# The two additions that complete the scores, as TensorE products into the bank of the transposed scores

## The chip, the cores and the metric

The kernel runs on one core of a Trainium2 chip. The metric is the time of one execution on the device, in microseconds, and the figure that counts is the median of several executions. In the profile, PE is TensorE (PEld its loading of the stationary operand), DVE is VectorE, ACT is ScalarE, POOL is GpSimd, and SP is the queue that issues most plain DMAs.

## The reference

Two graph layers over 3327 nodes with 128 features. The adjacency matrix is a mask times random weights, about 64 entries in a row, symmetric in its pattern. Layer 0 is a graph attention with four heads, and nearly all the time goes into it:

```python
def _gatv2_head(x, A_shape, w1, w2, a, Wlin):
    x1 = x @ w1
    x2 = x @ w2
    E = leaky_relu(x1[:, None, :] + x2[None, :, :], negative_slope=0.01)
    s = E @ a
    s = tanh(s / 8.0) * 8.0
    s = exp(s) * A_shape
    s = s / sum(s, axis=-1)
    out = s @ x @ Wlin.T
    return leaky_relu(out, negative_slope=0.01)

h = maximum(layernorm(x), 0);  x = x + concat(heads(h), axis=-1) @ w      # layer 0
h = maximum(layernorm(x), 0);  x = x + relu(A_norm @ (h @ W.T + b))        # layer 1
```

The score of a pair of nodes (i, j) in a head splits into a part with a relu and two plain terms: `leaky_relu(u) = 0.01 u + 0.99 relu(u)` with `u = x1[i] + x2[j]`, so `s = 0.99 a.relu(u) + 0.01 a.x1[i] + 0.01 a.x2[j]`. The last two are one number for each (j, head) and one for each (i, head). The change is about how these two numbers are added before the tanh.

## The kernel before, in words

**Tiling.** Rows are padded to 3328 and taken in 26 blocks of 128. A block is done in two halves (`hb`) of 64 rows. For each row the positions of its neighbours are found first, by `prep(b, k)`, and the neighbours' rows of a table in DRAM are then gathered. A half has four *words* `w` of eight tiles (`WT = 8`; a tile `g[:, t]` has 128 partitions, one pair (i, j) in each, with the features of j, the four plain terms of j at column `f0 + D`, and `x2[j]` for the four heads), and one *overflow word* (`w == NW`, three tiles, `ge`) for rows with more neighbours. That makes 26 x 2 x 5 = 260 words, 208 full ones and 52 overflow ones.

**Stages of a word.** `stage_z` works in groups `m` of four tiles, two groups to a full word: TensorE transposes the gathered `x2[j]` into PSUM (L622, 16 transposes for a group, in two halves `hp` of two heads), and VectorE takes the maximum with `-x1[i]` (L638, tile `r`). `stage_r` multiplies `r` with the attention vector on TensorE (L657): the relu parts of the scores stand in PSUM with pairs along the free axis. `finish` then turns scores into weights. It is a generator that does a piece of work, yields, and goes on at the next slot:

1. L666 ACT copies the scores to SBUF (`ssb`); L670 DVE makes `wq`.
2. Two slots later, L675: TensorE transposes `ssb` (four transposes of 128x128, three in an overflow word) into one bank `tr`, of which there are two for all users (`ps_tr`, `bufs=2`).
3. One slot later, L678: DVE adds to the transposed scores the plain term of j, which lies in `g`, into `sc` in SBUF; L681: DVE adds the term of i, which is `k.pex` in a full word and a part of `k.ex` in an overflow word.
4. Two slots later, L686 and L688: ACT takes tanh and exp of `sc`.
5. Two slots later, L697 (L715 in an overflow word): DVE multiplies by the adjacency weights into `wt`.
6. Five slots later, L706 (L724): TensorE accumulates `wt.T @ g` into `ag`, and `allow("g")` gives the gather buffer back to POOL's queue (L595).

`k.pex` is made once for a block at the end of `prep`: L561 DVE spreads the terms of i into `pmx` (each row's term under a mask), L566 TensorE multiplies with `modsel`, a 0/1 matrix that brings each row's term to the partitions of its pairs, and L568 ACT copies the product to SBUF.

**Order.** The instruction streams are written out in the order in which the Python code calls them (`manual_schedule`), and each engine runs its own stream in order. `slot()` is called six times for each group: before the group, after each half of the transposes of each `hp`, and after `stage_r`. Each call steps every open `finish` and `close` by one yield, steps `prep` of the next block at a fixed pace (72 steps in a block's 108 slots), and lets POOL issue gathers. So the DVE stream holds, between two of the L638 operations, whatever the slots between them put there. A PE instruction that waits holds up all PE instructions behind it, and the same goes for the other engines.

**L622 and its banks.** `z` has two buffers of two banks each, one for either `hp`. The transposes of one `hp` may start when L638 of the same `hp` one group earlier has read its bank.

The parts that the change touches: `prep` from L560 to L570, `finish` from L672 to L688.

Of the kernel before, what the change touches and what calls it, by code (L numbers as in the profile page):

```python
# [9 lines left out]
F32 = mybir.dt.float32  # L10
AF = mybir.ActivationFunctionType
OP = mybir.AluOpType
# [3 lines left out]
P = 128  # L16
SLOPE = 0.01
CAP = 8.0
# [44 lines left out]
OVT = 3  # L63
# [168 lines left out]
def _sparse_layers(tc, nc, x, adj, w1, w2, a, wlin, w, gw, gb, gb_sb, gwT, x_sb, dinv, flag, ident, out):  # L232
# [13 lines left out]
    NP, D = x.shape  # L246
    H = w1.shape[0]
# [5 lines left out]
    WT = 8  # L253
    NW = NT // WT
    LATE = 1

    with ExitStack() as l0:
# [19 lines left out]
        modsel = res.tile([P, P], F32, name="modsel")  # L277
# [8 lines left out]
        pb = l0.enter_context(tc.tile_pool(name="pb", bufs=2))  # L286
# [41 lines left out]
        def bank():  # L328
            return ps_tr.tile([P, 4, P], F32, name="tr").rearrange("p a b -> p (a b)")
# [23 lines left out]
        def prep(b, k):  # L353
# [114 lines left out]
            pm = bank()  # L468
# [27 lines left out]
            pm = bank()  # L496
# [22 lines left out]
            pm = bank()  # L519
            ex_ps = pm[:, :2 * OVT * 46].rearrange("p (t c) -> p t c", c=46)  # L520
            for c in range(2):
                for t in range(FOUND):
                    nc.tensor.matmul(ex_ps[:, OVT * c + t, :], oi[:, (FOUND * c + t) * P:(FOUND * c + t + 1) * P], ext[:, :46],
                                     start=True, stop=True)
# [25 lines left out]
            pm = bank()  # L550
            nc.tensor.matmul(pm, hTb, w1_sb.rearrange("p h d -> p (h d)"), start=True, stop=True)
            x1b = pb.tile([P, H * D], F32, name="x1b")
            nc.scalar.copy(x1b, pm)
            yield
            pm = bank()
            for h in range(H):
                nc.tensor.matmul(pm[:, h * P:(h + 1) * P], w1_sb[:, h, :], hTb, start=True, stop=True)
            x1n = pb.tile([P, H, P], F32, name="x1n")
            nc.scalar.activation(x1n, pm[:, :H * P].rearrange("p (h i) -> p h i", h=H), AF.Copy, scale=-1.0)
            pmx = pb.tile([P, 16, H], F32, name="pmx", bufs=1)  # L560
            nc.vector.tensor_tensor(pmx, tmask[:, :, None].to_broadcast([P, 16, H]),  # L561
                                    p_all[:, b, None, :H].to_broadcast([P, 16, H]), OP.mult)
            yield
            yield
            pm = bank()
            nc.tensor.matmul(pm[:, :16 * H], modsel, pmx.rearrange("p t h -> p (t h)"), start=True, stop=True)  # L566
            pex = pb.tile([P, 16, H], F32, name="pex")
            nc.scalar.copy(pex, pm[:, :16 * H].rearrange("p (t h) -> p t h", h=H))  # L568
            k.x1b, k.x1n, k.pex = x1b, x1n, pex
            yield  # L570

        def rows_in():
# [88 lines left out]
        def finish(k, hb, w):  # L661
            g, s = k.g.pop((hb, w)), k.s
            f0 = k.f0[hb]
            nt, nk, nm = (WT, 4, 2) if w < NW else (OVT, OVT, 1)
            ssb = ph.tile([P, BANK], F32, name="ssb", bufs=1)
            nc.scalar.copy(ssb[:, :nk * P], s[:, :nk * P])  # L666
            if w < NW:
                wq = pb.tile([P, WT, 8], F32, name="wq")
                diag = bass.AP(g.tensor, g.offset + BODY * hb, [list(g.ap[0]), [WIDE + 8, 8], [1, 8]])
                nc.vector.tensor_tensor(wq, diag, qmask[:, None, :].to_broadcast([P, WT, 8]), OP.mult)  # L670
            yield
            yield  # L672
            pt = ps_tr.tile([P, 4, P], F32, name="tr")
            for q in range(nk):
                nc.tensor.transpose(pt[:, q, :], ssb[:, q * P:(q + 1) * P], ident)  # L675
            yield
            sc = pb.tile([P, WT, H], F32, name="sc")
            nc.vector.tensor_tensor(sc[:, :nt].rearrange("p (m k) h -> p m k h", m=nm),  # L678
                                    pt.rearrange("p k (h m) -> p m k h", m=32)[:, :nm, :nk],
                                    g[:, :, f0 + D:f0 + D + H].rearrange("p (m k) h -> p m k h", m=nm), OP.add)  # L680
            nc.vector.tensor_add(sc[:, :nt], sc[:, :nt], k.pex[:, 8 * hb:8 * hb + 8] if w < NW else  # L681
                                 k.ex[:, OVT * hb:OVT * hb + OVT, 42:42 + H])
            yield
            yield
            th = pb.tile([P, WT, H], F32, name="th")
            nc.scalar.activation(th[:, :nt], sc[:, :nt], AF.Tanh, scale=1.0 / CAP)  # L686
            pe = pb.tile([P, WT, H], F32, name="pe")
            nc.scalar.activation(pe[:, :nt], th[:, :nt], AF.Exp, scale=CAP)  # L688
            yield
            yield  # L690

            if w == 0:
                k.ag = ps_a.tile([P, 2, 256], F32, name="ag")
            ag = k.ag
            if w < NW:
                wt = pv.tile([P, WT, H, 8], F32, name="wt", bufs=2)
                nc.vector.tensor_tensor(wt, pe[:, :, :, None].to_broadcast([P, WT, H, 8]),  # L697
                                        wq[:, :, None, :].to_broadcast([P, WT, H, 8]), OP.mult)
                yield
                yield  # L700
                yield
                yield
                yield
                for t in range(WT):
                    u, cg = t // 4, t % 4
                    nc.tensor.matmul(ag[32 * cg:32 * cg + 32, u, :WORK], wt[:, t].rearrange("p h q -> p (h q)"),  # L706
                                     g[:, t, f0:f0 + WORK], start=(w == 0 and t < 4), stop=False, skip_group_check=True)
                allow("g")
                return
            am = pb.tile([P, OVT, HALF], F32, name="am", bufs=1)  # L710
            wo = pv.tile([P, OVT, 8, H, 8], F32, name="wo")
            for t in range(OVT):
                nc.vector.scalar_tensor_tensor(am[:, t, :], code[:, :HALF], k.ex[:, OVT * hb + t, 41:42], g[:, t, BODY * hb:BODY * hb + HALF],
                                               op0=OP.is_equal, op1=OP.mult)
                nc.vector.tensor_tensor(wo[:, t], pe[:, t, None, :, None].to_broadcast([P, 8, H, 8]),  # L715
                                        am[:, t].rearrange("p (g q) -> p g q", q=8)[:, :, None, :].to_broadcast([P, 8, H, 8]), OP.mult)
                yield
            yield
            yield
            yield  # L720
            yield
            for t in range(OVT):
                for u in range(2):
                    nc.tensor.matmul(ag[:, u, :WORK], wo[:, t, 4 * u:4 * u + 4].rearrange("p g h q -> p (g h q)"),  # L724
                                     g[:, t, f0:f0 + WORK], start=False, stop=(t == OVT - 1), skip_group_check=True)
            allow("ge")
            tails.append(close(k, hb))
# [75 lines left out]
        for b in range(NB):  # L803
            k = Blk()
# [6 lines left out]
        SLOTP = 6 * 2 * NG  # L811
        AHEAD = 0.5
        preps = [prep(b, blks[b]) for b in range(NB)]
        queue = deque()
        done = [0] * NB
# [29 lines left out]
        def allow(kind):  # L845
            state[kind] += 1
# [345 lines left out]
        with tc.manual_schedule():  # L1192
# [5 lines left out]
            def scores(i):  # L1198
                if 0 <= i < n:
                    b, hb, m = groups[i]  # L1200
                    stage_r(blks[b], hb, m, rs.pop(i))
                    if m % 2 or m == NG - 1:
                        ends.append(finish(blks[b], hb, m // 2))
                    slot()

            for i in range(-1, n + 1):
                if i + 1 < n:
                    slot()
                if 0 <= i < n:
                    b, hb, m = groups[i]  # L1210
# [153 lines left out]
```

## Time and profile before

| | us |
|---|---|
| median of 9 runs | 3395.31 |
| lowest and highest of the 9 | 3378.94, 3409.59 |
| the profiled execution, its time | 3405.43 |
| its span, from the first to the last instruction | 3403.7 |
| PE matmul, busy | 2621.2 (77%) |
| DVE, busy | 2101.5 (62%) |
| ACT, busy | 682.7 (20%) |
| POOL, busy | 1714.7 (50%) |
| granted TensorE clock, mean | 0.887 |

How to read it: the profile has each instruction's start and duration by engine, source line and tile. A busy PE is the union of the matmuls' times, and a matmul's end is modelled, so of a run of matmuls the distance between starts tells what one takes in the stream, and the time of one (some 270 ns at full clock) is the way through the array. An fp32 matmul that isn't a transpose is two passes, each with its own load of the stationary operand, and is counted as two. The granted clock is either full or half over stretches of 3.4 us and more; the 0.887 is their mean. The chain is followed back from the last instruction to whatever released each, so its shares say which work the end waited for.

Over most of the span the picture is even: in 300 us stretches from 400 to 3100 us, PE is busy for 228 to 236 us, DVE for 184 to 196 us and ACT for 57 to 66 us.

### The profile page before, as it was taken

What the parts mean: (1) busy time and instruction counts of PE and PEld (TensorE: products, weight loads), DVE (VectorE), ACT (ScalarE), POOL (GpSimd) and SP (SyncE); (2) the same over time, 40 slices, a digit from 0 to 9 for tenths busy, and PEclk for the clock granted to TensorE, in tenths of its full rate; (3) what the DMA queues carried; (4) which work ended last, traced back from release to release, by engine and by line L of the source; (5) the groups of instructions that cost most, each with busy time, mean ns of one, the idle gap of its engine ahead of it and who ended that gap; (6) DMA issues with size and microseconds to landing.
All of it is one profiled execution on the core that took longest, in us unless ns stands there. A gap on an engine that the chain in (4) does not pass through costs nothing.

```text
span 3403.7 us, 52385 instructions
## 1 busy us (share of the span) xinstructions
PE 2621.2 (77%) x19410; PEld 1829.9 (54%) x19410; DVE 2101.5 (62%) x6426; ACT 682.7 (20%) x1703; POOL 1714.7 (50%) x1822
## 2 busy tenths in 40 slices
PE   6587777777887877777777777677777777787887
PEld 4355545555554555555555555555555555555543
DVE  6576666666666666666666665665665665665442
ACT  3122122112211212211221121221221121121110
POOL 3555555555455555545545545545555455445530
PEclk8798888888888989988888988988898888888999
DMA  9977677678677777877767867767777776777886
GB/s 324 320 252 259 207 259 255 217 243 281 211 240 260 239 234 257 262 215 247 257 196 251 269 202 246 258 205 242 249 229 230 240 227 219 247 219 228 257 281 186
DMA packets 417844, 826.94 MB, mean 243 GB/s; under 512 B 38435, under 2 KB 288815, under 8 KB 414255
## 3 DMA queue, kind: packets, MB, share of 16 engines
q0 software_dynamic: 141440, 619.41, 55.7%
q1 hardware_dynamic: 165343, 147.87, 14.0%
q10 hardware_dynamic: 110800, 56.25, 5.6%
q8 instruction: 156, 2.56, 0.3%
q14 instruction: 105, 0.86, 0.1%
HBM read 754.47 MB, written 113.22 MB: 255 GB/s over the span
## 4 chain that ended last, share of the span: by engine, by line
PE 50%; DVE 18%; issue 11%; another core or an unknown queue 11%; DMA 5%; POOL 4%; ACT 1%; SPq 0%; ACTq 0%; DVEq 0%; POOLq 0%
PE z L622 18%; PE s L657 10%; DVE r L638 9%; PE ag L706 4%; POOL g L595 4%; PE z L627 3%; PE tr L675 2%; DMA g<-table,idx 2%; DVE cand L422 2%; PE ag L724 2%; PE tr L379 2%; DVE codes L410 1%; PE z L988 1%; PE tr L757 1%
## 5 line engine op out<-in xcount | busy, mean ns | idle before, releaser
L595 POOL DMA_INDIRECT g<-table,idx x1664 | 1590.0, 956 | 1371.9 <-PE ag L706 802.2
L638 DVE TENSOR_TENSOR r<-z,x1n 128x1024 f32<-128x1024 f32 x832 | 1013.1, 1218 | 854.0 <-remote 341.7
L622 PE MATMUL z<-ident,g 128*128 128x128 f32 x6656 | 1044.6, 301 | 184.6 <-issue 117.3
L622 PEld LDWEIGHTS z<-ident,g 128*128 128x128 f32 x6656 | 850.8, 156 | 366.2 <-issue 236.0
L657 PE MATMUL s<-r,sel 128*2 128x512 f32 (+1 forms) x3744 | 552.7, 608 | 135.5 <-DVE r L638 91.6
L666 ACT COPY ssb<-s 128x512 f32<-128x512 f32 x260 | 146.9, 565 | 842.1 <-PE s L657 305.1
L706 PE MATMUL ag<-g,wt 128*32 128x133 f32 x3328 | 233.6, 307 | 95.2 <-issue 94.4
L657 PEld LDWEIGHTS s<-r,sel 128*2 128x2 f32 x3744 | 82.8, 84 | 411.2 <-issue 272.7
L706 PEld LDWEIGHTS ag<-g,wt 128*32 128x32 f32 x3328 | 134.1, 118 | 213.8 <-issue 204.4
L675 PE MATMUL tr<-ident,ssb 128*128 128x128 f32 x988 | 169.1, 296 | 92.5 <-issue 72.7
L422 DVE MAX8 cand<-codes 128x8 f32<-128x52 uint16 x1664 | 217.3, 204 | 0.0
L675 PEld LDWEIGHTS tr<-ident,ssb 128*128 128x128 f32 x988 | 127.2, 153 | 117.9 <-issue 93.3
L595 POOL DMA_INDIRECT ge<-table,idxo x104 | 101.1, 972 | 170.4 <-PE ag L724 81.3
L379 PE MATMUL tr<-at,x_sb 128*128 128x128 f32 x488 | 97.9, 357 | 113.9 <-ACT at L367 103.5
L367 ACT COPY at<-tr 128x512 f32<-128x512 f32 (+1 forms) x175 | 97.3, 556 | 409.4 <-remote 208.0
L686 ACT ACTIVATE th<-sc 128x32 f32<-128x32 f32 x260 | 58.4, 225 | 516.6 <-DVE sc L681 259.4
L379 PEld LDWEIGHTS tr<-at,x_sb 128*128 128x128 f32 x488 | 82.2, 252 | 141.6 <-ACT at L367 122.9
L633 DVE TENSOR_TENSOR r<-z,x1n 128x128 f32<-128x128 f32 x104 | 30.2, 290 | 192.3 <-PE z L627 140.7
L365 PE MATMUL tr<-ident,adjb 128*128 128x128 f32 x676 | 123.8, 311 | 27.7 <-DMA adjb<-in_adj_dram 16.3
L627 PE MATMUL z<-oi,x1b 128*128 128x256 f32 x416 | 133.2, 404 | 4.6 <-issue 4.6
L453 DVE MAX8 lists<-cand 128x8 f32<-128x272 f32 (+1 forms) x338 | 133.2, 394 | 2.2
L622 PE MATMUL z<-ident,ge 128*128 128x128 f32 x416 | 87.7, 286 | 43.0 <-issue 32.7
(199 smaller groups left out, 2611.1 us busy)
## 6 DMA issues: line engine op xcount, KB each, us to landing
adjb<-in_adj_dram SPq DMA_DIRECT2D x26, 1664.0 KB
table<-AT_d SPq DMA_DIRECT2D x26, 1664.0 KB
AT_d<-at ACTq DMA_DIRECT2D x150, 256.0 KB
g<-table,idx POOLq DMA_INDIRECT x1664
table<-img SPq DMA_DIRECT2D x12, 1296.0 KB
adjb<-AT_d SPq DMA_DIRECT2D x72, 128.0 KB
g<-AT_d SPq DMA_DIRECT2D x25, 256.0 KB
g<-AT_d ACTq DMA_DIRECT2D x25, 256.0 KB
```

Of the source, the lines that this page charges most:

```text
L365: nc.tensor.transpose(pt[:, q, :], adjb[:, (j0 + q) * P:(j0 + q + 1) * P], ident)
L379: nc.tensor.matmul(pq[:, :P], x_sb[:, j0 + q, :], at[:, q, :], start=(q == 0), stop=(q == js[-1]))
L422: nc.vector.max(cand[:, c, 8:].rearrange("p (r s) -> p r s", s=32)[:, :, sgm % 32], codes.rearrange("p a b -> p (a b)")[:, sgm % 32 * SEG: ...
L453: nc.vector.max(top, of)
L595: return nc.gpsimd.indirect_dma_start(out=g[:, t, lo:hi], out_offset=None, in_=tab, in_offset=bass.IndirectOffsetOnAxis(ap=at[:, t:t + 1], ...
L622: nc.tensor.matmul(z[:, i, q * P:(q + 1) * P], g[:, m % 2 * 4 + q, c0:c0 + D], ident, is_transpose=True, start=(q == 0 or m < 8), stop=(m ...
L627: nc.tensor.matmul(z[:, i, :n], k.x1b[:, h * D:(h + 1) * D], k.oi[:, hb * n:(hb + 1) * n], start=False, stop=True, skip_group_check=True)
L638: nc.vector.tensor_tensor(r.rearrange("p h (i s) -> p h i s", s=16), z.rearrange("p h (i s) -> p h i s", s=16), k.x1n[:, 2 * hp:2 * hp + 2 ...
L657: nc.tensor.matmul(k.s[32 * h:32 * h + 2, :n], sel[:, h, 31 - at:33 - at], r[h // 2][:, h % 2, :n], start=(at == 0), stop=(at == 1 or m == 8))
L666: nc.scalar.copy(ssb[:, :nk * P], s[:, :nk * P])
L675: nc.tensor.transpose(pt[:, q, :], ssb[:, q * P:(q + 1) * P], ident)
L706: nc.tensor.matmul(ag[32 * cg:32 * cg + 32, u, :WORK], wt[:, t].rearrange("p h q -> p (h q)"), g[:, t, f0:f0 + WORK], start=(w == 0 and t ...
```

## The change

The two DVE additions L678 and L681 and the tile `sc` go. In their place two products on TensorE accumulate into the bank that holds the transposed scores: identity times the terms of j (a strided view of `g`), and `modsel` times `pmx` for the terms of i (identity times the part of `k.ex` in an overflow word). Each writes 32 columns (12 in an overflow word) at the places of the bank where the valid scores stand. The four transposes become matmuls with `is_transpose`, of which the first clears the bank's state and the others and the products accumulate. Tanh reads the bank with the strided view and writes `th` dense. Of the three yields between the transposes and tanh, one is left: tanh, and all that follows in `finish`, stands two slots earlier in the streams.

In `prep` the product with `modsel`, its copy to SBUF (`pex`) and two yields go; `pmx` itself is kept for the block and has two buffers in place of one.

```diff
-            pmx = pb.tile([P, 16, H], F32, name="pmx", bufs=1)
+            pmx = pb.tile([P, 16, H], F32, name="pmx")
             nc.vector.tensor_tensor(pmx, tmask[:, :, None].to_broadcast([P, 16, H]),
                                     p_all[:, b, None, :H].to_broadcast([P, 16, H]), OP.mult)
-            yield
-            yield
-            pm = bank()
-            nc.tensor.matmul(pm[:, :16 * H], modsel, pmx.rearrange("p t h -> p (t h)"), start=True, stop=True)
-            pex = pb.tile([P, 16, H], F32, name="pex")
-            nc.scalar.copy(pex, pm[:, :16 * H].rearrange("p (t h) -> p t h", h=H))
-            k.x1b, k.x1n, k.pex = x1b, x1n, pex
+            k.x1b, k.x1n, k.pmx = x1b, x1n, pmx
...
             pt = ps_tr.tile([P, 4, P], F32, name="tr")
             for q in range(nk):
-                nc.tensor.transpose(pt[:, q, :], ssb[:, q * P:(q + 1) * P], ident)
-            yield
-            sc = pb.tile([P, WT, H], F32, name="sc")
-            nc.vector.tensor_tensor(sc[:, :nt].rearrange("p (m k) h -> p m k h", m=nm),
-                                    pt.rearrange("p k (h m) -> p m k h", m=32)[:, :nm, :nk],
-                                    g[:, :, f0 + D:f0 + D + H].rearrange("p (m k) h -> p m k h", m=nm), OP.add)
-            nc.vector.tensor_add(sc[:, :nt], sc[:, :nt], k.pex[:, 8 * hb:8 * hb + 8] if w < NW else
-                                 k.ex[:, OVT * hb:OVT * hb + OVT, 42:42 + H])
-            yield
+                nc.tensor.matmul(pt[:, q, :], ssb[:, q * P:(q + 1) * P], ident, is_transpose=True, start=(q == 0), stop=False,
+                                 skip_group_check=True)
+            sc = pt.rearrange("p k (h m) -> p m k h", m=32)[:, :nm, :nk]
+            parts = [(ident, g[:, :nt, f0 + D:f0 + D + H])]
+            if w < NW:
+                parts.append((modsel, k.pmx[:, 8 * hb:8 * hb + 8]))
+            else:
+                parts.append((ident, k.ex[:, OVT * hb:OVT * hb + OVT, 42:42 + H]))
+            for at, (by, term) in enumerate(parts):
+                nc.tensor.matmul(sc, by, term.rearrange("p (m k) h -> p m k h", m=nm), start=False, stop=(at == 1), skip_group_check=True)
             yield
             th = pb.tile([P, WT, H], F32, name="th")
-            nc.scalar.activation(th[:, :nt], sc[:, :nt], AF.Tanh, scale=1.0 / CAP)
+            nc.scalar.activation(th[:, :nt].rearrange("p (m k) h -> p m k h", m=nm), sc, AF.Tanh, scale=1.0 / CAP)
```

## The prediction, made before the changed kernel was run

> **What bounds the kernel now.** First the page's busy times and the shares of the chain that ended last:
>
> ```profile
> PE 2621.2 (77%) x19410; PEld 1829.9 (54%) x19410; DVE 2101.5 (62%) x6426; ACT 682.7 (20%) x1703; POOL 1714.7 (50%) x1822
> ...
> PE 50%; DVE 18%; issue 11%; another core or an unknown queue 11%; DMA 5%; POOL 4%; ACT 1%; SPq 0%; ACTq 0%; DVEq 0%; POOLq 0%
> PE z L622 18%; PE s L657 10%; DVE r L638 9%; PE ag L706 4%; POOL g L595 4%; PE z L627 3%; PE tr L675 2%; DMA g<-table,idx 2%; DVE cand L422 2%; PE ag L724 2%; PE tr L379 2%; DVE codes L410 1%; PE z L988 1%; PE tr L757 1%
> ```
>
> No engine is full, but half of the chain is PE work and less than a fifth is DVE work. Then the list of waits, to see who holds whom:
>
> ```profile
> DVE r L638 <- remote: 341.7, 105, 6.8
> ...
> DVE r L638 <- PE z L622: 297.0, 170, 5.5
> ...
> ACT th L686 <- DVE sc L681: 259.4, 91, 10.1
> ...
> PEld z L622 <- DVE r L638: 111.1, 141, 4.3
> ```
>
> (columns: us in total, times, longest). DVE stands 297 us before L638 for TensorE's transposes; PE stands 111 us before those transposes for L638. The two feed each other through the two `z` buffers, and PE is more often the one that is late. ACT's 259 us before tanh cost nothing by themselves: ACT is idle 80% of the span. The gathers do not bound: PE stands 1.7 us for them before L622, so a buffer given back sooner is worth nothing.
>
> Third, what the change removes, and its nearest kin on PE, from the groups by line and shape (busy us, mean ns of one, idle before):
>
> ```profile
> L675 PE MATMUL tr<-ident,ssb 128*128 128x128 f32 x988 | 169.1, 296 | 92.5 <-issue 72.7 <-ACT ssb L666 16.2 <-DMA g<-table,idx 3.5
> ...
> L681 DVE TENSOR_TENSOR sc<-sc,pex 128x32 f32<-128x32 f32 x208 | 40.0, 192 | 7.2
> L678 DVE TENSOR_TENSOR sc<-tr,g 128x32 f32<-128x32 f32 x208 | 38.5, 185 | 44.4 <-remote 22.0 <-PE tr L675 8.2 <-PE ag L724 3.7
> ...
> L566 PE MATMUL tr<-pmx,modsel 128*128 128x64 f32 x52 | 11.3, 300 | 0.0
> ...
> L681 DVE TENSOR_TENSOR sc<-sc,ex 128x12 f32<-128x12 f32 x52 | 8.9, 171 | 1.8
> L678 DVE TENSOR_TENSOR sc<-tr,ge 128x12 f32<-128x12 f32 x52 | 8.7, 167 | 27.8 <-remote 13.3 <-PE tr L675 7.9 <-DMA g<-table,idx 4.5
> ```
>
> Fourth, the timeline of weight loads, for what a pass takes in the stream. Starts are what counts:
>
> ```profile
> 1591.23 0.47 PEld L675 LDWEIGHTS tr<-ident,ssb 128*128 128x128 f32 x4
> 1591.67 0.97 PEld L768 LDWEIGHTS tr<-w_sb,outT 128*128 128x128 f32 x8
> ```
>
> ```profile
> 1672.11 0.83 PEld L675 LDWEIGHTS tr<-ident,ssb 128*128 128x128 f32 x4
> 1672.92 1.13 PEld L622 LDWEIGHTS z<-ident,g 128*128 128x128 f32 x10
> ```
>
> In the first pair four passes take 0.44 us, 0.110 each; in the second, at half clock, 0.81, so 0.203. The granted mean of 0.887 means half clock in (1 - 0.887) / 0.5 = 22.6% of the time, so a mean pass takes 0.774 x 0.110 + 0.226 x 0.203 = 0.131 us.
>
> **Added: the products.** Each is an fp32 matmul with a full 128x128 stationary operand, two passes, as the x52 for 26 calls of L566 shows. Two products to a word: 4 passes x 260 words = 1040 passes. A pass with few columns is not cheaper than one with 128: L470, with 16 columns, stands in the chain as eight passes in 0.80 us at full clock, 0.100 each, so the load sets the price. I take 0.131, as L675 is the neighbour: 136 us of PE stream. Bounds: 0.100 gives 104 us, L566's busy time per pass (11.3 / 52 = 0.217, with the way through the array in it) gives 226.
>
> How much of it is on the path? The products follow at once on L675, so I give them L675's own share of the chain. Adding up the pieces of the chain over the span, L675 has 78.4 us, of 988 x 0.131 = 129 us of stream: 61%. So +136 x 0.61 = +83 us. The other 39% lies where PE would next stand for L638 anyway.
>
> No row of before shows a matmul that writes separated columns of a bank; these write one float in 32. I let it cost nothing beside the load of the next pass, and cover it with the upper bound above. A page of the Trainium skill speaks against the change here: "PSUM — Partial Sum Buffer", section "Specifications (TRN2)", says that PSUM's lines are 8 bytes and that a non-contiguous access pattern slows matmuls significantly. It gives no figure and no run shows one yet. If that doubled each pass, the sum by it would be another 83 us.
>
> **Removed from PE.** L566, 52 passes: 7.0 us of it are on the chain. -7. Its copy L568 is on an idle ACT: 0.
>
> **Removed from DVE.** L678 and L681, 520 instructions: 38.5 + 8.7 + 40.0 + 8.9 = 96.1 us. The chain holds 12.6 us of L678 and 14.0 of L681, added up the same way: 26.6, or 28%. The rest is DVE time in which L638 had nothing to read yet. -27.
>
> With them goes a wait: DVE stands 44.4 + 27.8 = 72.2 us before L678 with the next L638 queued behind it. 35.3 of it (22.0 + 13.3) has no known releaser and will turn up before another instruction; 36.9 at most could come off. This wait moves to tanh on ACT, where little stands behind it. L638 often needs transposes that stand behind the same L675, so I take 0 and keep -37 for the range.
>
> **Moved.** The PE stream of the changed kernel has the `ag` products of a full word (L706) before the last four transposes of an `hp` and the L657 batch, in place of behind L657. POOL's gathers wait for them and come two slots earlier, into a queue that is not late. What was behind L657 covered the copy `ssb`: between L657 and L675 stand now eight transposes alone, some 0.45 us less. Going through the 208 full words, L675 starts a median 0.66 us after its `ssb` ended; the shortfalls under 0.45 us sum to 13 us. On the other side PE stands 135 us before L657 in 63 gaps for L638, and up to 0.45 us of each, 25 us in all, can now be filled by `ag`. Between -25 and +13: taken as 0. L697 (`wt`) moves forward past one L638 on DVE and can wait there for exp, which stands behind the products; that L638 feeds a score batch only a group later, so 0. The bank `tr` is held until tanh in place of L678: 4 passes more, without DVE's queue, 0. No DMA is added; those of POOL come earlier, and SP's keep their order.
>
> **Sum.** +83 - 7 - 27 = +49 us, against the profiled execution's 3405.4: 3454. It stands 10 us above the median of the runs (3395.3), so I predict a median of 3444. By the two prices of a pass: 104 x 0.61 - 34 = +29 and 226 x 0.61 - 34 = +104, and with the 37 of DVE's wait off the lower: 3387 to 3499 is the forecast's own range.
>
> **Rivals.**
>
> *DVE's relief outweighs the products (faster).* The place is the stretch from L675 to the next L638. If PE's passes there fall into the time in which DVE is the late one, they get the chain share that the additions had, 28%: 136 x 0.28 = +38; off come 7, 27 and the 37 of the wait before L678: -33, so 3362. It decides once less than (34 + 37) / 136 = 52% of the products is on the path. For it: PE stands 111 us before L622 for L638, and in the chain at 2409 to 2412 us L638, L678, L681 and the selection of neighbours follow each other on DVE without a gap. Against it: DVE has only 18% of the chain, and waits for PE more than PE for DVE.
>
> *Nothing hides the products (much slower).* Each pass is paid in full, and the lost cover of `ssb` too: 136 + 13 - 34 = +115, so 3510. For it: PE with "issue" is 61% of the chain, and a late transpose makes L638, its bank and the next transpose late in turn. Against it: PE stands idle for 23% of the span.
>
> *It does not matter (the same).* Relief and load cancel, 83 against 34, 37 and the 25 that `ag` may fill: about 3395. For it: both engines have some 9 us of work in the 13.1 us of a word (3404 / 260), so each is often the other's cover.
>
> **How the numbers follow.** The forecast has 0.48, the faster rival 0.22, the full price 0.18, no change 0.12. The predicted time is the forecast's, 3444. The range goes from the faster rival's price to the full price, with a little on both: 3360 to 3515. A measurement of this kernel tells 0.3%, 10 us, from no change. Faster by more than that 0.22, within it 0.12, slower 0.66.
>
> **What would show it.** The products as 1040 more passes behind the transposes of `ssb`, their starts 0.11 apart at full clock; more than 0.15 would mean that the separated columns cost. DVE's busy time down by 96 us and PE's up by about 130. Idle of PE before L622 for L638 down, and of DVE before L638 for PE up, if PE is the path; the reverse of the second if the faster rival holds. Idle before L675's successor for `ssb` up by 13 us at most. The prediction is wrong if the products' starts stand in what was idle PE time, or if the granted clock moves: each 0.01 of it is worth some 1.1% of the chain's 50% PE, 19 us.

## The result, and the profile after

The changed kernel takes 3753.7 us, the median of 14 runs, against 3399.9 of the kernel before beside it: a ratio of 1.103, with an interval from 1.101 to 1.105. The prediction was 3444 with a range up to 3515. The sign was right, the size was not: 354 us were lost, not 49. In some groups of the runs below the kernel before itself took some 2500 us and in the others 3280 to 3420, for a reason that no run names, so every ratio is to the kernel before in the same group, and the two conditions are kept apart as "the 2500" and "the 3400".

In the profile after, the page's busy times and the chain that ended last:

```profile
PE 2805.0 (75%) x20398; PEld 1960.4 (52%) x20398; DVE 2034.3 (54%) x5906; ACT 667.4 (18%) x1677; POOL 1700.9 (45%) x1822
...
PE 59%; another core or an unknown queue 14%; issue 10%; DVE 8%; ACT 4%; DMA 3%; POOL 1%; ACTq 0%; SPq 0%; DVEq 0%
PE z L616 20%; PE s L651 12%; DVE r L632 5%; PE ag L701 5%; PE z L621 3%; PE tr L669 2%; PE ag L719 2%; PE tr L678 2%; PE tr L379 2%; PE tr L365 2%; ACT ssb L660 1%; PE tr L551 1%; PE z L983 1%; DVE codes L410 1%
```

PE has 184 us more of busy time, but it also stands idle for longer: the gaps of PE with its weight loads sum to 936 us, where they were 754. VectorE has 67 us less to do and idles 427 us more. The span grew by 360 us (3403.7 to 3763.5): 182 of idle time on PE, and 178 of time in which it works or loads. The busy half isn't the added products alone: the granted clock fell from 0.887 to 0.84, and the transposes of `z`, which the change doesn't touch, are busy for 1119.9 us in place of 1044.6. So half of the loss is waiting; PE's share of the chain goes from 50 to 59%, that of DVE from 18 to 8.

For what? The groups by line and shape (busy us, mean ns of one, idle time before them and what ended it). The lines have moved: the transposes of `ssb`, L675 before, are now L669; `wt` is L692 and `ag` L701.

```profile
L616 PE MATMUL z<-ident,g 128*128 128x128 f32 x6656 | 1119.9, 314 | 302.5 <-issue 155.4 <-DVE r L632 144.4 <-DMA g<-table,idx 2.0
...
L701 PE MATMUL ag<-g,wt 128*32 128x133 f32 x3328 | 191.3, 366 | 0.0
L669 PE MATMUL tr<-ident,ssb 128*128 128x128 f32 x988 | 167.4, 293 | 233.6 <-ACT ssb L660 194.9 <-issue 38.3
...
L692 DVE TENSOR_TENSOR wt<-pe,wq 128x256 f32<-128x256 f32 x208 | 87.9, 422 | 254.1 <-issue 129.5 <-ACT pe L683 88.3 <-ACT th L681 35.2
L678 PE MATMUL tr<-pmx,modsel 128*128 128x32 f32 x416 | 82.9, 282 | 0.0
...
L678 PE MATMUL tr<-g,ident 128*128 128x32 f32 x416 | 65.5, 240 | 0.0
```

Before the change, three of these groups read:

```profile
L622 PE MATMUL z<-ident,g 128*128 128x128 f32 x6656 | 1044.6, 301 | 184.6 <-issue 117.3 <-DVE r L638 64.6 <-DMA g<-table,idx 1.7
...
L706 PE MATMUL ag<-g,wt 128*32 128x133 f32 x3328 | 233.6, 307 | 95.2 <-issue 94.4
...
L697 DVE TENSOR_TENSOR wt<-pe,wq 128x256 f32<-128x256 f32 x208 | 86.4, 416 | 3.3 <-ACT pe L688 3.3
```

The idle time before the transposes of `ssb` was 92.5 us and is 233.6, most of it (194.9, where it was 16.2) for ACT's copy. Before the transposes of `z` it grew by 118 us. Before `wt`, VectorE waited 3 us and now 254. The 95 us that PE stood before `ag` are gone. The two products of a full word are the 832 passes of L678, none with idle time before it.

The list of waits (us in total, times, longest) names the same places:

```profile
PEld z L616 <- DVE r L632: 316.8, 122, 6.4
...
DVE r L632 <- PE z L616: 238.4, 162, 4.9
PEld tr L669 <- ACT ssb L660: 210.9, 65, 4.8
...
PEld tr L779 <- ACT th L681: 104.8, 22, 5.9
```

The first was 111.1 us and the second 297.0 before: of the waits that the list can name, PE's for VectorE's maximum are now the longer ones. (Another 408.8 us before the maximum stand as "remote", 341.7 before the change; the last section says what these are.) The last is new: 1.5 us before. L779 transposes the centred rows of layer 1's input in `close`; it needs a bank `tr`, and the bank is freed by tanh. One such place in the timeline (start, duration, engine):

```profile
1769.11 0.60 PE L616 MATMUL z<-ident,g 128*128 128x128 f32 x4
...
1769.54 0.60 PE L669 MATMUL tr<-ident,ssb 128*128 128x128 f32 x4
...
1770.12 0.39 PE L678 MATMUL tr<-pmx,modsel 128*128 128x32 f32 x2
...
1774.31 1.23 DVE L632 TENSOR_TENSOR r<-z,x1n 128x1024 f32<-128x1024 f32 x1 [2.39 <-PE z L616]
...
1777.20 0.20 ACT L681 ACTIVATE th<-tr 128x32 f32<-128x32 f32 x1 [4.39 <-remote]
...
1777.44 0.18 PEld L779 LDWEIGHTS tr<-ident,agn 128*128 128x128 f32 x1 [4.58 <-ACT th L681]
```

The last product of the word ends at 1770.51 by the profile's modelled end, tanh starts at 1777.20, and PE stands until 1777.44 with all its later work behind L779. The 6.7 us between the product's end and tanh have no cause that the trace names; more of that at the end.

### The profile page after: what moved, and what is told of

Read it like the earlier page. It is cut to its first block, busy times and chain, and to the rows that moved or that the text cites. A ratio compares the mean times of both kernels' runs of the same rounds, so it can differ in the third digit from the quotient of the medians.

```text
span 3763.5 us, 53741 instructions
## 1 busy us (share of the span) xinstructions
PE 2805.0 (75%) x20398; PEld 1960.4 (52%) x20398; DVE 2034.3 (54%) x5906; ACT 667.4 (18%) x1677; POOL 1700.9 (45%) x1822
## 4 chain that ended last, share of the span: by engine, by line
PE 59%; another core or an unknown queue 14%; issue 10%; DVE 8%; ACT 4%; DMA 3%; POOL 1%; ACTq 0%; SPq 0%; DVEq 0%
PE z L616 20%; PE s L651 12%; DVE r L632 5%; PE ag L701 5%; PE z L621 3%; PE tr L669 2%; PE ag L719 2%; PE tr L678 2%; PE tr L379 2%; PE tr L365 2%; ACT ssb L660 1%; PE tr L551 1%; PE z L983 1%; DVE codes L410 1%
## 5 line engine op out<-in xcount | busy, mean ns | idle before, releaser
L632 DVE TENSOR_TENSOR r<-z,x1n 128x1024 f32<-128x1024 f32 x832 | 1012.3, 1218 | 703.8 <-remote 408.8
L616 PE MATMUL z<-ident,g 128*128 128x128 f32 x6656 | 1119.9, 314 | 302.5 <-issue 155.4
L616 PEld LDWEIGHTS z<-ident,g 128*128 128x128 f32 x6656 | 913.5, 166 | 528.5 <-issue 350.2
L651 PE MATMUL s<-r,sel 128*2 128x512 f32 (+1 forms) x3744 | 515.9, 610 | 26.5 <-issue 21.4
L669 PE MATMUL tr<-ident,ssb 128*128 128x128 f32 x988 | 167.4, 293 | 233.6 <-ACT ssb L660 194.9
L669 PEld LDWEIGHTS tr<-ident,ssb 128*128 128x128 f32 x988 | 119.0, 147 | 262.2 <-ACT ssb L660 210.9
L651 PEld LDWEIGHTS s<-r,sel 128*2 128x2 f32 x3744 | 80.0, 85 | 298.0 <-issue 288.7
L692 DVE TENSOR_TENSOR wt<-pe,wq 128x256 f32<-128x256 f32 x208 | 87.9, 422 | 254.1 <-issue 129.5
L616 PE MATMUL z<-ident,ge 128*128 128x128 f32 x416 | 103.9, 339 | 142.4 <-DVE r L632 138.0
L701 PE MATMUL ag<-g,wt 128*32 128x133 f32 x3328 | 191.3, 366 | 0.0
L681 ACT ACTIVATE th<-tr 128x32 f32<-128x32 f32 x260 | 50.4, 194 | 789.4 <-remote 377.8
L616 PEld LDWEIGHTS z<-ident,ge 128*128 128x128 f32 x416 | 55.3, 164 | 217.2 <-DVE r L632 145.6
L621 PE MATMUL z<-oi,x1b 128*128 128x256 f32 x416 | 150.4, 449 | 0.0
L701 PEld LDWEIGHTS ag<-g,wt 128*32 128x32 f32 x3328 | 104.7, 137 | 73.5 <-issue 67.0
```

The lines of the kernel that those rows point to most:

```text
L616: nc.tensor.matmul(z[:, i, q * P:(q + 1) * P], g[:, m % 2 * 4 + q, c0:c0 + D], ident, is_transpose=True, start=(q == 0 or m < 8), stop=(m ...
L621: nc.tensor.matmul(z[:, i, :n], k.x1b[:, h * D:(h + 1) * D], k.oi[:, hb * n:(hb + 1) * n], start=False, stop=True, skip_group_check=True)
L632: nc.vector.tensor_tensor(r.rearrange("p h (i s) -> p h i s", s=16), z.rearrange("p h (i s) -> p h i s", s=16), k.x1n[:, 2 * hp:2 * hp + 2 ...
L651: nc.tensor.matmul(k.s[32 * h:32 * h + 2, :n], sel[:, h, 31 - at:33 - at], r[h // 2][:, h % 2, :n], start=(at == 0), stop=(at == 1 or m == 8))
L669: nc.tensor.matmul(pt[:, q, :], ssb[:, q * P:(q + 1) * P], ident, is_transpose=True, start=(q == 0), stop=False, skip_group_check=True)
```

## The experiments

The first group of runs (`b4`, `c7`, `early_adds`, `load`) and the last two (`only_ag` to `only_ag_again`) fell in the 2500, the others in the 3400, where the result above was taken too. Several expectations name times or ranges for the other condition than the one that the run met; such a range decides nothing.

### Where the places stand: b4 and c7

Both keep the products and give back places. Two yields are added; in `b4` ahead of `wt`, so that `wt` and `ag` stand where they stood before, in `c7` behind `wt`, so that `ag` alone does.

```diff
# b4
             nc.scalar.activation(pe[:, :nt], th[:, :nt], AF.Exp, scale=CAP)
             yield
             yield
+            yield
+            yield
# c7
                 yield
                 yield
+                yield
+                yield
                 for t in range(WT):
```

> The changed kernel with two more yields between exp and wt: tanh and exp stay where the change put them, wt (DVE) and the ag products (PE) go back to their old places in the streams. Theory 'places': most of the loss comes from wt, which stands 254 us idle on DVE before it with L632 (the maximum) queued behind, and from ag, which no longer covers the ssb copy (PE idle before the transposes of ssb 92 before, 233 after): those go, and the price of the products is left, 3500 to 3570. Theory 'load': the products themselves and the bank they hold cost it, and the places matter little: 3680 or more.

> The changed kernel with two more yields between wt and ag: only the ag products go back behind the score batch, wt stays early. Theory 'places': PE's idle before the transposes of ssb goes from 233 back towards 92 us, the idle of DVE before wt stays near 254: 3620 to 3680. If wt alone makes the loss, 3730 or more; if ag alone makes it, below 3580. Theory 'load': 3730 or more.

Measured, in the 2500: `b4` 0.996 [0.9945, 0.9976], `c7` 1.000 [0.9986, 1.0017]. Later, with the changed kernel beside them:

> The changed kernel with two more yields between exp and wt, once more: its first measurement (0.996) fell where the kernel before took 2502 us. If the kernel before takes about 3400 us here: theory 'places' says that wt and ag at their old places leave the products' price alone, as in the experiment with zero products (1.032): 1.025 to 1.045. Theory 'load and bank' (tanh holds the bank longer, PE waits for it): 1.07 or more. If it takes about 2500 us: 0.996 again.

> The changed kernel with two more yields between wt and ag, once more (first 1.000 at 2502 us). At about 3400 us: if ag in front of the score batch makes the loss, the products' price is left, 1.025 to 1.045, with wt early; if wt in front of the maximum makes it (266 us of DVE idle before wt), 1.07 to 1.11; a half each, near 1.065. At about 2500 us: 1.000 again.

> The changed kernel beside the three. At about 3400 us: 1.10 to 1.11 again. At about 2500 us: theory 'ag' says the loss of early additions (1.064) less what the products gain there (the two variants with old ag were at 0.996 and 1.000): 1.04 to 1.07.

Measured, in the 3400 (before: 3278.5): `b4_again` 1.0285 [1.023, 1.0339], `c7_again` 1.028 [1.0225, 1.0334], the changed kernel 1.122 [1.1168, 1.1279]. So one edit of two yields, which moves the `ag` products of the full words behind the score batch (and with them the moment at which their gather buffer is given back) and nothing else, takes away 306 of 404 us (3682.2 to 3376.3). That `c7` and `b4` are alike says that the earlier `wt` costs nothing once `ag` stands in its old place. `c7_again` also shows what the expectation had otherwise: VectorE's idle time before `wt` doesn't stay near 254 us but falls to 54.5, so most of it came with the place of `ag` too.

The groups of `c7_again`, and then of the changed kernel beside it:

```profile
L669 PE MATMUL tr<-ident,ssb 128*128 128x128 f32 x988 | 161.4, 286 | 56.4 <-issue 51.3 <-ACT ssb L660 4.0 <-DVE cand L422 0.8
...
L692 DVE TENSOR_TENSOR wt<-pe,wq 128x256 f32<-128x256 f32 x208 | 87.0, 418 | 54.5 <-ACT pe L683 43.8 <-ACT th L681 4.3 <-issue 3.9
...
L781 PE MATMUL tr<-ident,agn 128*128 128x128 f32 x26 | 7.1, 275 | 0.3 <-ACT agn L776 0.3
```

```profile
L669 PE MATMUL tr<-ident,ssb 128*128 128x128 f32 x988 | 170.0, 296 | 234.7 <-ACT ssb L660 202.5 <-issue 32.1
...
L779 PE MATMUL tr<-ident,agn 128*128 128x128 f32 x26 | 11.6, 448 | 108.5 <-issue 71.7 <-ACT th L681 36.6 <-ACT agn L774 0.2
```

Both long waits of PE go with the place of `ag`: 178 us before the transposes of `ssb` and 108 before L779. Tanh stands at the same early slot in both kernels, so the bank held until tanh doesn't make the second wait by itself. Between the two spans (3375.8 and 3677.5) PE's idle time grows by 178 us, from 701 to 879 (some other gaps shrink), and the time in which it works or loads by 124: together the 302.

### The places without the products: early_adds, no_products

`early_adds` leaves the two additions on VectorE and takes two yields away, so that tanh and all behind it stand two slots earlier, as in the changed kernel. `no_products` is the changed kernel without its products; it leaves the plain terms out of the scores.

```diff
# early_adds, against the kernel before
-            yield
-            yield
             th = pb.tile([P, WT, H], F32, name="th")
# no_products, against the changed kernel
-            for at, (by, term) in enumerate(parts):
+            for at, (by, term) in enumerate(()):
```

> The kernel before, with its two DVE additions and pex, but with the two yields between the additions and tanh left out: tanh, exp, wt and ag stand two slots earlier, as in the changed kernel, and PE has no products. Theory 'places': a loss of about half to two thirds of the change's 354 us, 3550 to 3650. Theory 'load': 3380 to 3430.

> The kernel before with tanh, exp, wt and ag two slots earlier, its DVE additions kept, once more (first 1.064 at 2502 us). At about 3400 us: theory 'places' says 1.06 to 1.09, as the changed kernel without its products (1.070). Theory 'load and bank': below 1.02. At about 2500 us: 1.064 again.

> The changed kernel without its two products: tanh reads the transposed scores alone, so the plain terms of i and j are left out of the scores. All places are those of the changed kernel. Theory 'ag': the loss stays but for the products' own price: 0.015 to 0.03 below the changed kernel. Theory 'load': at or below the kernel before, 0.96 to 1.00.

> The changed kernel once more, beside the others: in the first four experiments the kernel before took 2502 us in place of 3400, so the change has to be measured where they are. Theory 'ag' (the loss comes from the ag products standing in front of the score batch): 1.04 to 1.08 of the kernel before, as the experiment with early additions (1.064). Theory 'late completions' (the loss exists only where completions of PE reach the other engines microseconds late, which the slow traces show and the fast ones don't): 0.99 to 1.02.

> The kernel before once more, for its profile in these conditions. Both theories: ratio 1.00. Granted clock above 0.96 and completions of PE picked up within 0.1 us, if its time is near 2500 us.

Measured, in the 2500: `early_adds` 1.064 [1.0604, 1.0677]. In the 3400: `early_adds_again` 1.081 [1.0753, 1.0862]; `no_products` 1.070 [1.0639, 1.0757], beside the changed kernel with 1.107 [1.1014, 1.1128] and the kernel before against itself with 1.003 [0.9991, 1.0062]. The places without the products lose 7% (`no_products`); the products on top of them are worth 0.037, a little over the 0.015 to 0.03 expected. `early_adds` isn't the same case, though its 8% is near: with the additions on VectorE, tanh and `wt` come right behind them, and in the 2500 it lost four times as much as `ag` moved by itself (`only_ag`, below). Why it does stays open, so it isn't counted as evidence for the places of the changed kernel.

### The products without the places: load, load_dense

Two products that add zeros go behind the four transposes in the kernel before; all else stays. In `load` they write the separated columns, in `load_dense` as many neighbouring ones. `nil` is a tile of zeros that is made once; the line for `load_dense` stands in place of the last two of `load`.

```diff
# load, against the kernel before
-                nc.tensor.transpose(pt[:, q, :], ssb[:, q * P:(q + 1) * P], ident)
+                nc.tensor.matmul(pt[:, q, :], ssb[:, q * P:(q + 1) * P], ident, is_transpose=True, start=(q == 0), stop=False,
+                                 skip_group_check=True)
+            for at, by in enumerate((ident, modsel if w < NW else ident)):
+                nc.tensor.matmul(pt.rearrange("p k (h m) -> p m k h", m=32)[:, :nm, :nk], by,
+                                 nil[:, :nt].rearrange("p (m k) h -> p m k h", m=nm), start=False, stop=(at == 1), skip_group_check=True)
# load_dense, against load
+                nc.tensor.matmul(pt[:, 0, :nt * H], by, nil[:, :nt].rearrange("p t h -> p (t h)"), start=False, stop=(at == 1), skip_group_check=True)
```

> The kernel before, with all its places and its DVE additions, and two products with a zero moving operand added into the bank of the transposed scores right after the transposes: the change's PE load (1040 passes, the same stationary operands, the same separated columns) alone; the zeros change no value. Theory 'places': 3400 plus 61 to 100% of 136 us, 3480 to 3540. Theory 'load': 3650 or more.

> The experiment with zero products in the kernel before, with the products written to 32 neighbouring columns in place of 32 columns 32 apart. If separated columns slow a product, this is faster than that one (1.0145) by 0.005 or more and the starts of the products are closer; if they don't, 1.012 to 1.017 and the same starts. Only the two products per word differ.

Measured: `load` 1.0145 [1.0113, 1.0177] in the 2500, 36 us; `load_dense` 1.032 [1.0254, 1.0379] in the 3400, 108 us by the ratio (the two medians lie 99 apart). The two totals come from different conditions and say nothing of the columns. The weight loads in the timeline do, first `load`, then `load_dense`:

```profile
1653.61 0.30 PEld L680 LDWEIGHTS tr<-nil,ident 128*128 128x128 f32 x2
1653.83 0.30 PEld L680 LDWEIGHTS tr<-nil,modsel 128*128 128x128 f32 x2
1653.97 0.50 PEld L624 LDWEIGHTS z<-ident,g 128*128 128x128 f32 x4
```

```profile
1655.33 0.30 PEld L680 LDWEIGHTS tr<-nil,ident 128*128 128x128 f32 x2
1655.55 0.30 PEld L680 LDWEIGHTS tr<-nil,modsel 128*128 128x128 f32 x2
1655.69 0.83 PEld L624 LDWEIGHTS z<-ident,g 128*128 128x128 f32 x7
```

From the first load of the products to the load that follows them it is 0.36 us for four passes in both, 0.09 a pass. The median over the 208 full words is the same in the two kernels to the nanosecond. Separated columns cost nothing here, with 32 of them to a product.

### ag by itself, and which way it costs: only_ag, c6, cover

`only_ag` is the kernel before with nothing moved but `ag`, two slots earlier. `c6` is the changed kernel with `ag` one slot later: directly in front of the score batch, no longer between two lots of four transposes. `cover` keeps `ag` in its early place and puts the transposes of `ssb` a slot later.

```diff
# only_ag, against the kernel before; five yields become three
                 yield
                 yield
                 yield
-                yield
-                yield
                 for t in range(WT):
# c6, against the changed kernel; five become six
+                yield
                 for t in range(WT):
# cover, against the changed kernel; one more here, and five become four between wt and ag
+            yield
             pt = ps_tr.tile([P, 4, P], F32, name="tr")
```

> The kernel before with one edit: two of the five yields between wt and the ag products go, so that the ag products of a word stand two slots earlier, between the last two groups of four transposes before the score batch (L657), and nothing else in the word moves. Theory A, the place of ag alone makes the lost time of places: 1.06 to 1.08 of before, like early_adds_again (1.081) and no_products (1.070), with PE idle up by 120 us or more. Theory B, the place of tanh and wt has a part in it: 1.02 to 1.05.

> The changed kernel with one more yield between wt and ag: the ag products stand behind all eight transposes and directly in front of the score batch, so the transposes of ssb are as bare of cover as in the changed kernel, but no transposes of z stand behind the ag products. Theory C, the loss is the lost cover of the copy ssb: as the changed kernel beside it, 1.09 to 1.12 (less the idle time before the other instructions, a few tens of us), and PE's idle time before the transposes of ssb stays at 200 us or more. Theory D, the loss is that the second four transposes, and with them L632 on VectorE, come 2 us later: 1.03 to 1.05, with the idle time before the transposes of z falling back towards the 174 us of before.

> The changed kernel with the transposes of ssb and the products one slot later, and one yield less between wt and ag, so that ag keeps the place that it has in the changed kernel. Between the score batch and the transposes of ssb no ag products stand, but the place where they wait lies behind one more slot (that before the next group, in which prep's and close's instructions of TensorE may stand; no transposes of z). Theory C: the idle time before the transposes of ssb falls below 150 us and the ratio by 0.03 or more against the changed kernel beside it. Theory D: within 0.02 of the changed kernel, idle time before the transposes of z still 250 us or more.

> The changed kernel once more, as the yardstick of this group: 1.10 to 1.12 of before if the conditions are those of most runs; about 1.03 to 1.06 if the kernel before takes some 2500 us here.

> c6 once more, hoping for the slower conditions. If the kernel before takes 3280 to 3420 us here: theory D 1.03 to 1.05, about as c7_again (1.028) and b4_again (1.0285); theory C 1.09 to 1.12. If it takes some 2500 us again: 0.998 as in c6.

> only_ag once more. If the kernel before takes 3280 to 3420 us here: 1.06 to 1.08 if the place of ag alone makes the loss of places, 1.02 to 1.05 if tanh and wt have a part. If it takes some 2500 us again: 1.016 as in only_ag.

All six ran in the 2500 (before: 2499.2 and 2499.6). `only_ag` 1.0159 [1.0141, 1.0178] and again 1.0148 [1.0119, 1.0176]; the changed kernel 1.0168 [1.015, 1.0185]; `cover` 1.023 [1.0214, 1.0249]; `c6` 0.998 [0.997, 0.9994] and again 0.996 [0.9952, 0.9976]. The first ranges for theories A to D were written for the 3400, and none was met in full; the changed kernel too lost less than the 1.03 to 1.06 expected of it here.

Here `only_ag` and the changed kernel are 3 us apart (2537.3 and 2540.4): the place of `ag` is the whole loss, and the products pay for themselves. Theory C, the lost cover of `ssb`, has nothing to explain in these conditions: `c6` leaves `ssb` as bare as the changed kernel does and loses nothing, `cover` gives it room and gains nothing, and PE hardly waits there at all, first in the changed kernel (`after_fourth`), then in `c6`:

```profile
L669 PE MATMUL tr<-ident,ssb 128*128 128x128 f32 x988 | 151.8, 274 | 12.4 <-ACT ssb L660 12.4
```

```profile
L669 PE MATMUL tr<-ident,ssb 128*128 128x128 f32 x988 | 151.9, 275 | 10.7 <-ACT ssb L660 10.5
```

Theory D named the right edit, but its reason doesn't carry the 46 us between the changed kernel and `c6` (2540.4 and 2494.3): PE's idle time differs by only 12 us (184 and 172), 9 of it before the transposes of `z`. The other 34 us are busy time (2334.8 and 2301.0), with the same instructions. The timeline of PE shows where, first in `after_fourth`, the changed kernel, then in `c6`:

```profile
1097.53 0.60 PE L616 MATMUL z<-ident,g 128*128 128x128 f32 x4
1098.06 0.66 PE L701 MATMUL ag<-g,wt 128*32 128x133 f32 x16
1098.65 0.66 PE L616 MATMUL z<-ident,g 128*128 128x128 f32 x4
1099.23 1.90 PE L651 MATMUL s<-r,sel 128*2 128x512 f32 x16
1101.07 0.66 PE L616 MATMUL z<-ident,g 128*128 128x128 f32 x4
```

```profile
604.12 0.60 PE L365 MATMUL tr<-ident,adjb 128*128 128x128 f32 x4
604.56 0.60 PE L616 MATMUL z<-ident,g 128*128 128x128 f32 x4
605.09 0.67 PE L702 MATMUL ag<-g,wt 128*32 128x133 f32 x16
605.57 1.90 PE L651 MATMUL s<-r,sel 128*2 128x512 f32 x16
607.40 0.66 PE L616 MATMUL z<-ident,g 128*128 128x128 f32 x4
```

Read the starts. Four transposes take 0.44 us where transposes follow, and 0.53 or 0.58 where products with few stationary columns (32 for `ag`, 2 for the scores) follow. The `ag` products take 0.59 where transposes follow and 0.48 where the score batch does. The stretch with eight transposes, one `ag` and one score batch takes 3.54 us in the first kernel; in the second 3.28 (604.12 to 607.40; four of its transposes are those of `adjb`, of the same shape). With `ag` by itself among transposes PE changes between the two kinds twice more for each word. The place is a fair one: over the whole trace the `ag` products take a median 0.59 us before transposes and 0.48 before the score batch. In the changed kernel the score batch follows directly on `ag` in 1 of the 208 full words, in `c6` in 155; in the others it is work with all 128 stationary columns. At 0.26 us, 154 words make 40 us, an estimate, for the 46 measured, of which 34 are busy time. The runs of the changed kernel's kin in the 2500 fit: those with `ag` next to the score batch (`b4`, `c7`, `c6` twice) are at 0.996 to 1.000, those with `ag` between transposes (`only_ag` twice, the changed kernel, `cover`) at 1.015 to 1.023. No run changes the order of the kinds without moving `ag`, so the changeover is read from the timeline and not tried by itself.

What `ag`'s early place does in the 3400 is shown as to the place, by `c7_again` against the changed kernel, but not as to the way: neither `c6` nor `only_ag` met those conditions. There the changeovers can be only a part of the 306 us. The rest is idle time, and a slower clock (0.902 in `c7_again`, 0.838 beside it). Whether that idle time comes from the lost cover of `ssb` or follows from the later transposes stays open.

## Why the prediction was wrong, step by step

- **The step that failed is "Moved".** It priced `ag` in front of the score batch between -25 and +13 us and took 0. The place of `ag` is worth 306 us in the 3400 and 46 in the 2500. Three things were missed. It counted gaps before L657 that `ag` might fill and the shortfall of the cover behind it from the old trace, as if the rest of that trace stayed where it was: "13 us at most" for `ssb` became 179 (16.2 to 194.9). The gaps before the score batch did shrink, from 135 us to 27 (10.7 and 15.8 in the two shapes of L651), but PE's waits came back before other instructions. It took PE's work to be the same in any order, where `ag` between transposes costs two changes more a word. And it took the clock to stay.
- **The clock.** The text gave 19 us for each 0.01. The clock went from 0.887 to 0.84 with the added idle time: some 89 us by that rule. In the trace of the kernel before, PE neither multiplies nor loads for more than 3.4 us 48 times, and after 46 of them begins a stretch at half clock, during the wait or within 3.5 us of its end; in the changed kernel it is 121 waits and 119 of them, and the time at half clock goes from 770 to 1204 us. The Trainium skill's page "TensorE: Matmul & The Clock Gate", section "HAM oscillation — how this bites in real kernels", says that idle gaps above about 3.4 us throttle the engine again. These counts agree, though such waits don't account for every half-clock stretch: the kernel before has 134, so 88 of them begin without one. A new long wait on PE is thus paid twice, as idle time and as a slower stretch behind it.
- **The products, +83.** Mis-sized a little: `load_dense`, which adds them alone, costs 108 us [87 to 129] in the 3400; from `no_products` to the changed kernel it is 119. The pass was cheaper than the 0.131 us taken, the share on the path higher than 61%: from the first load of the products to the load behind them, summed over the 260 words of `load_dense`, it is 108 us, 0.103 a pass, so about all of it was paid. (The loads themselves start 0.11 apart, as forecast.) In the 2500 `load` costs 36 us of 100, 0.096 a pass. The share isn't a property of the code; it moves with what else is late.
- **The separated columns, 0.** Right. The page "PSUM — Partial Sum Buffer", section "Specifications (TRN2)", has matmuls slowed significantly by a non-contiguous pattern; 0.09 us a pass for separated and neighbouring columns alike doesn't show it for these small fp32 products.
- **The additions and L566, -34, and DVE's wait, 0.** In the 3400 `c7_again` costs 0.028 x 3278.5 = 92 us with them removed and `load_dense` 108 with them kept: about 16 us between them, less than the width of either interval, so a gain of 34 isn't excluded and isn't shown. DVE's busy time fell by 67 us, not 96: the durations of its instructions sum to 100 us less, so about a third of what went had overlapped with other DVE instructions.
- **`wt` early, 0.** Right as to its price (`b4` and `c7` are the same); the wait before it is 54.5 us with `ag` in its old place and 254 with `ag` early. **The bank held until tanh, 0:** right where `ag` is in its old place (0.3 us before L781 in `c7_again`); with `ag` early PE waits 108 us there.
- **The sum without the places** was +49; the nearest run, `c7_again`, is at +92, inside the forecast's own range (3387 to 3499, which is -8 to +104 against the median of 3395). Of the rivals "Nothing hides the products" came nearest with 3510, but by the products' full price, where the loss was the place.

The prediction named the doubtful step and said how it could fail ("if the granted clock moves"), yet gave it no price from far above, as it did for the products. It also left the largest row of its own list of waits unread: the 341.7 us of "remote" before L638, of which 339.7 lie after the modelled end of the very transposes that L638 waits for.

## What to carry to other kernels

Yields taken out of a staged pipeline move every later stage; price the move by itself and try it by itself before the arithmetic is judged: here the two removed yields cost three times as much as the products in one set of conditions, and all of the loss in the other. On TensorE look at what stands beside a group of small-stationary products: here `ag` took 0.48 us in front of others of their kind and 0.59 in front of full-width transposes. With yields put back the change is 0 to 0.4% faster in one set of conditions (`b4`, `c6`, `c7`) and 2.8% slower in the other (`b4`, `c7`), so no version tried is better than the kernel before in both.

## What the hardware showed that wasn't expected

- The same kernel before took 2499 us in some groups and 3280 to 3420 in others, on one chip in both. In the kernels run in the faster groups PE is busy for 88 to 93% of the span at a clock of 0.96 to 0.985; the kernel before in the slower ones has 77% at 0.89.
- One difference in the traces is when VectorE goes on after PE is done. In the kernel before, in the 3400, L638 started a median 1.0 us after both the modelled end of its transposes and VectorE's own earlier work, over 387 waits of more than 0.15 us, 616 us in all; 340 us of it are the waits put down to "remote". In `only_ag`, in the 2500, it is 0.04 us in each of 187 such waits, and the same line is

```profile
L638 DVE TENSOR_TENSOR r<-z,x1n 128x1024 f32<-128x1024 f32 x832 | 1011.5, 1216 | 140.3 <-PE z L622 138.5
```

  with 140 us of idle time in place of 854.0, and no "remote" in it. What makes the completions late isn't settled. The place of `ag` cost 46 us where they are prompt and 306 where they are late; that the lateness makes this difference wasn't tried by itself.
- In the changed kernel in the 2500 the weight loads of the sixteen passes of `ag`, four of them side by side in 32 columns each, start 18 ns apart (in the median 276 ns from the first to the last). From the last weight load of the transposes before them to their first it is 0.31 us, where 0.11 lies between transposes, and from their last to the next transposes 0.32; where the score batch follows (`c6`) the second is 0.09.
